# A language adapter with residual layer norm: b2 shared out anew between VectorE and TensorE, and the negative means of two batches in one operation

## The chip, the cores and the metric

The kernel runs on one core of a Trainium2 chip. Its engines work side by side, each through its own instruction queue: TensorE (PE) multiplies matrices, VectorE (DVE) and ScalarE (ACT) work on vectors, GpSimd (POOL) does elementwise work, SyncE (SP) issues the DMAs. The metric is the device time of one execution in microseconds, the median of several runs.

## What is computed

There are 128 sequences ("batches" b) of 128 rows of 512 float32 values. Each has a language id that picks one of ten sets of weights.

```python
h = relu(x @ W1[id] + b1[id])              # 512 -> 128
adapted = h @ W2[id] + b2[id]              # 128 -> 512
y = x + adapted
normed = (y - mean(y)) * rsqrt(var(y) + 1e-05)
out = x + normed * gamma[id] + beta[id]
```

## The kernel before

All weights lie in SBUF from the start; the rows of b2, gamma and beta are spread over 128 partitions (`spread`, line 159). Then one Python loop (line 476), fully unrolled, runs over the steps i. Every engine has its own order of instructions, which is the order of the program: `keep` (line 43) ties each instruction to the one before it on its engine.

In step i, with b = i - 3, the engines work on different batches, as a pipeline:

- TensorE: `transpose_x(i)` (line 202, four transposes), `down(i-1)` (line 225, the first product, eight instructions), `up(i-2)` (lines 236 to 242, the second product, two instructions over 512 columns, into a PSUM tile of the pool `p_y`). `p_y` has five buffers (line 61), so the product of batch b takes the buffer that batch b-5 gave back with its `finish`.
- ScalarE: `copy_xT(i)` (L206), `stage_w1(i+1)` (L197), `relu(i-1)` (L233), `square(b)` (L272, the sum of squares about the mean, which needs the sum of the row), and after every odd b `deviation` (L283, the root of the variance for a pair of batches).
- GpSimd: `add_b2(b+2)` (L212, r = x + b2) and `add_beta(b)` (L219, o = x + beta), 1.28 us each.
- VectorE, in an even step b with g = b / 2 and p = g - 1: `residual(b)` (L257, y = y + r, with the sum of each row as a second result), `rstd_1(p)` (L289), `scale(2p)` (L306, (y - mean) * gamma), `negative_mean(b)` (L263), `rstd_2(p)` (L293), `finish(2p-1)` (L315, o = y * rstd + o), `rstd_3(p)` (L297). In an odd step: `residual(b)`, `rstd_4(p)` (L301), `scale(2p+1)`, `negative_mean(b)`, `finish(2p)`. So batch b-3 is finished in step b. The four `rstd` operations work on two columns, one for each batch of a pair; their results in between lie in a tile `stat` in PSUM (pool `p_s`).

b2 is added in one of three ways. In most batches GpSimd adds it to x (`add_b2`). Where `b2_by_matmul(b)` holds (line 188), TensorE puts it into the PSUM tile with one more matmul ahead of the second product (L241, from bfloat16 parts of the row). Where `b2_by_vector(b)` holds (line 191), VectorE adds it to the product in PSUM (L255) ahead of the residual. In the last two ways the residual takes x itself. Before, 22 batches go to TensorE (0 to 3, and every b with b % 8 == 1, and 5, 117 and 125), 13 to VectorE (b % 8 == 5 from 13 to 109), 93 to GpSimd.

Stores go out by pair of batches (`store`, L319), from SP's queue, which also issues the loads of x, four batches each (L67).

The last four batches (E = 123, so 124 to 127) have an order of their own, written out by hand in `tail` (line 380). There each batch has its own root and reciprocals (`deviation_of` L350 and L352, `rstd_of` with n = 1 to 4, L336, L339, L342, L345, one column each, all in one PSUM tile `stat_ends`). `by_pool` (L366 on ScalarE, L368 and L370 on GpSimd) ends batches 123, 124 and 125, for the first two with `shift` (L360) from the negative mean; `finish_last` (L377) ends 122, 126 and 127 on VectorE. Each is stored by itself (L373).

Of the kernel before, what the change touches and what calls it, by code (L numbers as in the profile page):

```python
# [8 lines left out]
FP = mybir.dt.float32  # L9
# [3 lines left out]
ALU = mybir.AluOpType  # L13
# [3 lines left out]
P = 128  # L17
# [6 lines left out]
def cond_resid_kernel(ctx: ExitStack, tc: tile.TileContext, x, itok, W1, b1, W2, b2, gamma, beta, out):  # L24
# [8 lines left out]
    nc = tc.nc  # L33
    B, S, H = x.shape
# [8 lines left out]
    def keep(ins):  # L43

        engine = ins.ins.engine
        if engine in last:
            tc.add_manual_dep(ins.ins, last[engine], behind, reason="kept order")
        last[engine] = ins.ins.name
        return ins
# [7 lines left out]
    st = ctx.enter_context(tc.tile_pool(name="st", bufs=6))  # L57
    p_x = ctx.enter_context(tc.tile_pool(name="p_x", bufs=1, space=PSUM))
    p_h = ctx.enter_context(tc.tile_pool(name="p_h", bufs=1, space=PSUM))
    p_s = ctx.enter_context(tc.tile_pool(name="p_s", bufs=1, space=PSUM))  # L60
# [109 lines left out]
    lids, xT, w1s, hT, rs, os, ys, ssqs, nmeans, rstds = {}, {}, {}, {}, {}, {}, {}, {}, {}, {}  # L170
    phs, pxs, sums = {}, {}, {}

    def lid(b, engine):
        g = b // G
        if (g, engine) not in lids:
            loads, vals = nc.values_load_multi_w_load_instructions(
                lang[0:1, g * G : (g + 1) * G],
                engines=[engine],
                min_val=0,
                max_val=L - 1,  # L180
                skip_runtime_bounds_check_because="clamped on the chip to 0..L-1 above",
            )
            for ins in loads:
                keep(ins)
            lids[g, engine] = vals
        return lids[g, engine][b % G]
# [2 lines left out]
        return b < 4 or (b % 4 == 1 and not b2_by_vector(b))  # L189

    def b2_by_vector(b):
        return b % 8 == 5 and 8 <= b < B - 16

    def stage_w1(b):
        w1s[b] = wp.tile([P, KC, A], FP, tag="w1s", name=f"w1s_{b}")
# [49 lines left out]
    def col(tiles, b):  # L245

        return tiles[b // 2][:, b % 2 : b % 2 + 1]

    def residual(b):
        r = rs.pop(b) if b in rs else xb(b)  # L250
        if b % 2 == 0:
            sums[b // 2] = st.tile([P, 2], FP, tag="sum", name=f"sum_{b // 2}")
        if b2_by_vector(b):
            v = lid(b, ET.DVE)
            keep(nc.vector.tensor_tensor(ys[b], ys[b], b2_b[:, bass.ds(v * H, H)], ALU.add))  # L255
        keep(
            nc.vector.scalar_tensor_tensor(ys[b], ys[b], 1.0, r, ALU.mult, ALU.add, accum_out=col(sums, b))  # L257
        )

    def negative_mean(b):  # L260
        if b % 2 == 0:
            nmeans[b // 2] = st.tile([P, 2], FP, tag="nmean", name=f"nmean_{b // 2}")
        keep(nc.vector.tensor_scalar(col(nmeans, b), col(sums, b), -1.0 / H, None, ALU.mult))  # L263

    def square(b):

# [10 lines left out]
    sds, y0s, stats = {}, {}, {}  # L277
# [7 lines left out]


    def rstd_1(g):
        y0s[g] = p_s.tile([P, 6], FP, tag="s", name=f"stat_{g}")
        keep(nc.vector.reciprocal(y0s[g][:, 0:2], sds[g]))  # L289

    def rstd_2(g):
        t = y0s[g]
        keep(nc.vector.scalar_tensor_tensor(t[:, 2:4], ssqs.pop(g), EPS * H3, t[:, 0:2], ALU.add, ALU.mult))  # L293
# [9 lines left out]
    def scale(b):  # L303
        v = lid(b, ET.DVE)
        keep(
            nc.vector.scalar_tensor_tensor(  # L306
                ys[b], ys[b], col(nmeans, b), gamma_b[:, bass.ds(v * H, H)], ALU.add, ALU.mult
            )
        )
# [8 lines left out]
    def store(g):  # L318
        nc.sync.dma_start(out=out[2 * g : 2 * g + 2].rearrange("b s h -> s b h"), in_=os.pop(g))  # L319
        del rstds[g]  # L320

    def on(b):
        return 0 <= b < B
# [4 lines left out]
    ends = {}  # L328

    def rstd_of(b, n):  # L330

        if not ends:
            ends["t"] = p_s.tile([P, 32], FP, tag="s", name="stat_ends")
        t = ends["t"][:, 8 * (b % 4) : 8 * (b % 4) + 3]
        if n == 1:
            keep(nc.vector.reciprocal(t[:, 0:1], sds[b]))  # L336
        elif n == 2:
            keep(
                nc.vector.scalar_tensor_tensor(t[:, 1:2], ssqs.pop(b), EPS * H3, t[:, 0:1], ALU.add, ALU.mult)  # L339
            )  # L340
        elif n == 3:
            keep(nc.vector.scalar_tensor_tensor(t[:, 2:3], t[:, 1:2], 1.0 / H3, sds.pop(b), ALU.mult, ALU.add))  # L342
        else:
            rstds[b] = st.tile([P, 1], FP, tag="rstd", name=f"rstd_{b}")
            keep(nc.vector.reciprocal(rstds[b], t[:, 2:3]))  # L345
# [9 lines left out]
    def rstd_col(b):  # L355
        return rstds[b] if b > E else rstds[b // 2][:, b % 2 : b % 2 + 1]
# [15 lines left out]
    def store_last(b):  # L372
        nc.sync.dma_start(out=out[b], in_=os[b // 2][:, b % 2, :])  # L373

    def finish_last(b):
        o = os[b // 2][:, b % 2, :]
        keep(nc.vector.scalar_tensor_tensor(o, ys.pop(b), rstd_col(b), o, ALU.mult, ALU.add))  # L377
        store_last(b)

    def tail(b):  # L380
        p = E // 2
        if b == E + 3:
            rstd_of(b - 2, 3)
        residual(b)
        if b == E + 1:
            rstd_1(p)
            scale(E - 1)
            rstd_2(p)
            negative_mean(b)
            finish(E - 2)  # L390
            store(p - 1)
            rstd_3(p)
            deviation_of(b)
            rstd_4(p)
            shift(E)
            by_pool(E, False)
        elif b == E + 2:
            rstd_of(b - 1, 1)
            negative_mean(b)
            rstd_of(b - 1, 2)  # L400
            finish_last(E - 1)
            store_last(E)
            deviation_of(b)
        elif b == E + 3:
            rstd_of(b - 2, 4)
            shift(b - 2)
            residual(b + 1)
            by_pool(b - 2, False)
            store_last(b - 2)
            rstd_of(b - 1, 1)  # L410
            negative_mean(b)
            rstd_of(b - 1, 2)
            negative_mean(b + 1)
            scale(b - 1)
            deviation_of(b)
            rstd_of(b - 1, 3)
            rstd_of(b - 1, 4)
            scale(b)
            deviation_of(b + 1)
            by_pool(b - 1, True)  # L420
            store_last(b - 1)
            rstd_of(b, 1)
            rstd_of(b, 2)
            rstd_of(b + 1, 1)
            rstd_of(b, 3)
            rstd_of(b + 1, 2)
            scale(b + 1)
            rstd_of(b, 4)
            rstd_of(b + 1, 3)
            rstd_of(b + 1, 4)  # L430
            finish_last(b)
            finish_last(b + 1)


# [41 lines left out]
    for i in range(3, B + U):  # L476
        b = i - U - 1
        if b > 0 and b % G == 0 and b // G + 3 < NG:
            load_x(b // G + 3)
        if i == 4:  # L480
            up(2)
        if i == 5:
            up(3)
        if i > 3 and on(i):
            transpose_x(i)
        if b <= E:
            add_b2(b + 2)
            add_beta(b)
        if i > 4 and on(i - 1):
            down(i - 1)  # L490
        if i > 3 and on(i):
            copy_xT(i)
        if i > 4 and on(i + 1):
            stage_w1(i + 1)
        if i > 4 and on(i - 1):
            relu(i - 1)
        if i > 5 and on(i - U):
            up(i - U)


        g, half = divmod(b, 2)
        p = g - 1
        mine, old = 0 <= p < B // 2, 0 <= p - 1 < B // 2
        if b == E:
            add_b2(b + 3)
            add_beta(b + 1)
            add_b2(b + 4)
            for n in range(b + 2, B):
                add_beta(n)
        if b > E:  # L510
            tail(b)
        elif half == 0:
            if on(b):
                residual(b)
            if mine:
                rstd_1(p)
                scale(2 * p)
            if on(b):
                negative_mean(b)
            if mine:  # L520
                rstd_2(p)
            if old:
                finish(2 * p - 1)
                store(p - 1)
            if mine:
                rstd_3(p)
        else:
            if on(b):
                residual(b)
            if mine:  # L530
                rstd_4(p)
                scale(2 * p + 1)
            if on(b):
                negative_mean(b)
            if mine:
                finish(2 * p)
        if 0 <= b <= E:
            square(b)
            if half == 1:
                deviation(g)  # L540

        for n, engine in ((i + 3, ET.Activation), (i - U + 3, ET.PE), (b + 1, ET.DVE), (b + 5, ET.Pool)):
            if on(n):
                lid(n, engine)
# [37 lines left out]
```

## Time and profile before

| | |
|---|---|
| median of 3 runs | 314.34 us (314.3 to 314.67) |
| the profiled execution | 314.2 us, its span 312.4 us |
| granted TensorE clock, mean | 0.989 |
| L241, b2 by matmul | 22 times |
| L255, b2 on VectorE | 13 times, 690 ns each |
| L263, negative mean | 128 times, 151 ns each |
| L257, residual | 128 times, 693 to 695 ns each |
| L306, scale | 126 times, 743 ns each |
| L315, finish | 122 times, 745 ns each |

The profile is one execution. Its page gives for each engine the busy time, the busy share in 40 equal slices of the span (a digit is tenths), and groups of instructions by line. The timeline gives the start of each instruction, its duration, engine, line and operation; instructions of one engine may overlap in it[...]. "PEld" is TensorE's loading of weights.

### The profile page before, as it was taken

To read this page: it belongs to the slowest core of one execution; us is meant where nothing else is said; L and a number is where in the kernel's file an instruction comes from. 1 tells how busy PE (TensorE), PEld (TensorE's weight loads), DVE (VectorE), ACT (ScalarE), POOL (GpSimd) and SP (SyncE) were. 2 spreads that over 40 slices of the span, in tenths; PEclk is the share of its full clock that TensorE was granted. 3 is DMA by queue.
4 is the path that set the end of the run, shared out by engine and by line. 5 is a ranking of instruction groups with operands and counts; after the bars stand their busy time and mean duration, and the time that the engine had idled before them with its cause. 6 is when DMAs were issued, how large, how long until landed. Compare 5 with 4: busy or idle time off the path is not lost.

```text
span 312.4 us, 7096 instructions
## 1 busy us (share of the span) xinstructions
PE 300.3 (96%) x1870; PEld 222.8 (71%) x1871; DVE 295.6 (95%) x943; ACT 285.8 (91%) x726; POOL 280.1 (90%) x234
## 2 busy tenths in 40 slices
PE   8999999999999999999999999999999999999980
PEld 3566777777777777777777777777777777777740
DVE  6827999999999999999999999999999999999995
ACT  3977999999999999999999999999999999999982
POOL 1307999999999999999999999999999999999964
PEclk9999999999999999999999999999999999999995
DMA  7998678677766667677666667787666667733244
GB/s 208 315 387 317 202 263 271 227 247 269 245 228 234 219 229 266 203 270 270 229 218 213 232 250 244 234 273 268 212 214 213 245 235 236 265 134 129 78 167 168
DMA packets 41001, 72.87 MB, mean 233 GB/s; under 512 B 1753, under 2 KB 6884, under 8 KB 40962
## 3 DMA queue, kind: packets, MB, share of 16 engines
q1 hardware_dynamic: 40902, 72.38, 67.2%
q8 instruction: 15, 0.25, 0.3%
q14 instruction: 24, 0.20, 0.2%
q10 hardware_dynamic: 60, 0.05, 0.1%
HBM read 38.86 MB, written 33.55 MB: 232 GB/s over the span
## 4 chain that ended last, share of the span: by engine, by line
PE 84%; DVE 4%; DMA 4%; SPq 3%; ACT 2%; issue 1%; DVEq 1%; ACTq 0%
PE ph L225 34%; PE py L242 33%; PE pxT L202 17%; DMA w<-in_L_cond_W_dram 4%; SPq L98 2%; PE py L241 1%; DVE py L257 1%; DVE py L306 1%; SPq L84 1%; DVE o L315 1%; ACT sq L350 0%; DVEq L577 0%; ACT xT L206 0%; ACT n L366 0%; ACT sq L272 0%
## 5 line engine op out<-in xcount | busy, mean ns | idle before, releaser
L219 POOL TENSOR_TENSOR o<-x,beta_b 128x512 f32<-128x512 f32 x128 | 162.2, 1280 | 9.1 <-ACT beta_b L166 9.1
L225 PE MATMUL ph<-xT,w1s 128*128 128x128 f32 x1024 | 135.6, 275 | 0.8 <-ACT w1s L197 0.5
L212 POOL TENSOR_TENSOR r<-x,b_b 128x512 f32<-128x512 f32 x93 | 118.9, 1279 | 15.9 <-DMA x<-in_x_dram 11.9
L242 PE MATMUL py<-w,hT 128*128 x256 | 131.2, 594 | 0.5 <-DMA w<-in_L_cond_W_dram 0.5
L225 PEld LDWEIGHTS ph<-xT,w1s 128*128 128x128 f32 x1024 | 124.6, 192 | 3.0 <-ACT hT L233 1.6
L202 PEld LDWEIGHTS pxT<-ident,x 128*128 128x128 f32 x512 | 63.7, 141 | 65.1 <-issue 45.9
L306 DVE SCALAR_TENSOR_TENSOR py<-py,nmean,gamma_b 128x512 f32<-128x512 f32 x126 | 93.6, 743 | 0.0
L315 DVE SCALAR_TENSOR_TENSOR o<-py,rstd,o 128x512 f32<-128x512 f32 x122 | 90.8, 745 | 0.0
L272 ACT ACTIVATE sq<-py,sum 128x512 f32<-128x512 f32 x124 | 85.2, 687 | 2.0 <-DVE py L257 1.8
L206 ACT COPY xT<-pxT 128x512 f32<-128x512 f32 x128 | 73.7, 576 | 9.4 <-PE pxT L202 5.8
L197 ACT COPY w1s<-w 128x512 f32 x128 | 79.3, 620 | 0.2 <-issue 0.2
L202 PE MATMUL pxT<-ident,x 128*128 128x128 f32 x512 | 76.8, 273 | 0.0
L257 DVE SCALAR_TENSOR_TENSOR py<-py,r 128x512 f32<-128x512 f32 x93 | 64.4, 693 | 1.4 <-issue 0.5
L233 ACT ACTIVATE hT<-ph,b1T 128x128 f32<-128x128 f32 x128 | 47.3, 370 | 1.2 <-PE ph L225 1.2
L242 PEld LDWEIGHTS py<-w,hT 128*128 128x128 f32 x256 | 40.5, 192 | 3.2 <-issue 1.6
L257 DVE SCALAR_TENSOR_TENSOR py<-py,x 128x512 f32<-128x512 f32 x35 | 24.3, 695 | 3.8 <-PE py L242 3.3
L272 ACT ACTIVATION_READ_ACCUMULATOR sq<-py,sum 128x1 f32 x124 | 25.6, 207 | 0.0
L283 ACT ACTIVATE sd<-ssq,eps 128x2 f32<-128x2 f32 x62 | 18.3, 296 | 2.1
L263 DVE TENSOR_SCALAR nmean<-sum 128x1 f32<-128x1 f32 x128 | 19.4, 151 | 0.1
L289 DVE RECIPROCAL stat<-sd 128x2 f32<-128x2 f32 x62 | 12.9, 208 | 1.1 <-ACT sd L283 1.1
L257 DVE DVE_READ_ACCUMULATOR py<-py,r 128x1 f32 x93 | 13.3, 143 | 0.0
L301 DVE RECIPROCAL rstd<-stat 128x2 f32<-128x2 f32 x62 | 10.3, 167 | 0.0
(55 smaller groups left out, 111.2 us busy)
## 6 DMA issues: line engine op xcount, KB each, us to landing
out_dram<-o SPq DMA_DIRECT2D x61, 512.0 KB, 3.2
x<-in_x_dram SPq DMA_DIRECT2D x30, 1024.0 KB, 6.0
w<-in_L_cond_W_dram SPq DMA_DIRECT2D x4, 640.0 KB, 6.3
w<-in_L_cond_W_dram SPq DMA_DIRECT2D x2, 1280.0 KB, 11.3
x<-in_x_dram SPq DMA_DIRECT2D x4, 512.0 KB, 8.2
out_dram<-o SPq DMA_DIRECT2D x6, 256.0 KB, 2.0
rows<-in_L_cond_beta_dram ACTq DMA_DIRECT2D x1, 20.0 KB
rows<-in_L_cond_gamma_dram SPq DMA_DIRECT2D x1, 20.0 KB
```

The lines of the kernel that those rows point to most:

```text
L197: keep(nc.scalar.copy(w1s[b].rearrange("p k a -> p (k a)"), src))
L202: keep(nc.tensor.transpose(pxs[b][:, k, :], xb(b)[:, k * P : (k + 1) * P], ident))
L206: keep(nc.scalar.copy(xT[b], pxs.pop(b)))
L212: keep(nc.gpsimd.tensor_tensor(rs[b], xb(b), b2_b[:, bass.ds(v * H, H)], ALU.add))
L219: keep(nc.gpsimd.tensor_tensor(os[g][:, j, :], xb(b), beta_b[:, bass.ds(v * H, H)], ALU.add))
L225: nc.tensor.matmul(phs[b], lhsT=w1s[b][:, k, :], rhs=xT[b][:, k, :], start=(k == 0), stop=(k == KC - 1))
L233: keep(nc.scalar.activation(hT[b], phs.pop(b), AF.Relu, bias=b1T[:, bass.ds(lid(b, ET.Activation), 1)]))
L242: keep(nc.tensor.matmul(ys[b], lhsT=hT[b], rhs=w2[:, bass.ds(v * H, H)], start=not m, stop=True))
L257: nc.vector.scalar_tensor_tensor(ys[b], ys[b], 1.0, r, ALU.mult, ALU.add, accum_out=col(sums, b))
L272: nc.scalar.activation(sq, ys[b], AF.Square, bias=col(sums, b), scale=-float(H), accum_out=col(ssqs, b))
L306: nc.vector.scalar_tensor_tensor(ys[b], ys[b], col(nmeans, b), gamma_b[:, bass.ds(v * H, H)], ALU.add, ALU.mult)
L315: nc.vector.scalar_tensor_tensor(o, ys.pop(b), rstds[g][:, j : j + 1], o, ALU.mult, ALU.add)
```

## The change

`b2_by_vector` holds now for b % 16 in 5, 9 and 13, from 9 to 109: 20 batches; `b2_by_matmul`, which takes what is left of b % 4 == 1, holds for 15. The 93 batches of GpSimd are the same ones.

`negative_mean(b)`, one operation on one column, becomes `negative_means(g)`, one on two columns, after the odd batch of a pair: sums * (-1/512) + 0. Its zeros are two columns of a new PSUM tile `small`, cleared once, in which all small results lie now: those of the pairs (`rstd_1`) in two places in turn, those of the last four batches in four others. `stat` and `stat_ends` are gone.

In `tail` the negative means of 124 and 125 are taken together in the turn of 125, and those of 126 and 127 between `rstd_of(125, 3)` and `rstd_of(125, 4)`. `scale(127)` goes ahead of `rstd_of(126, 2)`, and `finish_last(126)` ahead of `rstd_of(127, 4)`.

```diff
     def b2_by_vector(b):
-        return b % 8 == 5 and 8 <= b < B - 16
+        return b % 16 in (5, 9, 13) and 8 <= b < B - 16
...
-    def negative_mean(b):
-        if b % 2 == 0:
-            nmeans[b // 2] = st.tile([P, 2], FP, tag="nmean", name=f"nmean_{b // 2}")
-        keep(nc.vector.tensor_scalar(col(nmeans, b), col(sums, b), -1.0 / H, None, ALU.mult))
+    small = {}
+
+    def smalls(lo, n):
+        if not small:
+            small["t"] = p_s.tile([P, 64], FP, tag="s", name="small")
+            keep(nc.vector.memset(small["t"][:, 0:2], 0.0))
+        return small["t"][:, lo : lo + n]
+
+    def negative_means(g):
+        nmeans[g] = st.tile([P, 2], FP, tag="nmean", name=f"nmean_{g}")
+        keep(nc.vector.scalar_tensor_tensor(nmeans[g], sums[g], -1.0 / H, smalls(0, 2), ALU.mult, ALU.add))
...
     def rstd_1(g):
-        y0s[g] = p_s.tile([P, 6], FP, tag="s", name=f"stat_{g}")
+        y0s[g] = smalls(8 + 8 * (g % 2), 6)
...
     def rstd_of(b, n):
-        if not ends:
-            ends["t"] = p_s.tile([P, 32], FP, tag="s", name="stat_ends")
-        t = ends["t"][:, 8 * (b % 4) : 8 * (b % 4) + 3]
+        t = smalls(32 + 8 * (b % 4), 3)
...
         if b == E + 1:
             rstd_1(p)
             scale(E - 1)
             rstd_2(p)
-            negative_mean(b)
             finish(E - 2)
...
         elif b == E + 2:
             rstd_of(b - 1, 1)
-            negative_mean(b)
+            negative_means(b // 2)
             rstd_of(b - 1, 2)
...
             rstd_of(b - 1, 1)
-            negative_mean(b)
             rstd_of(b - 1, 2)
-            negative_mean(b + 1)
             scale(b - 1)
             deviation_of(b)
             rstd_of(b - 1, 3)
+            negative_means(b // 2)
             rstd_of(b - 1, 4)
             scale(b)
             deviation_of(b + 1)
             by_pool(b - 1, True)
             store_last(b - 1)
             rstd_of(b, 1)
+            scale(b + 1)
             rstd_of(b, 2)
             rstd_of(b + 1, 1)
             rstd_of(b, 3)
             rstd_of(b + 1, 2)
-            scale(b + 1)
             rstd_of(b, 4)
             rstd_of(b + 1, 3)
+            finish_last(b)
             rstd_of(b + 1, 4)
-            finish_last(b)
             finish_last(b + 1)
...
             if mine:
                 rstd_1(p)
                 scale(2 * p)
-            if on(b):
-                negative_mean(b)
-            if mine:
                 rstd_2(p)
...
             if on(b):
-                negative_mean(b)
+                negative_means(g)
             if mine:
                 finish(2 * p)
```

## The prediction

> **What bounds the kernel now.** I read the busy shares first, then the 40 slices.
>
> ```profile
> PE 300.3 (96%) x1870; PEld 222.8 (71%) x1871; DVE 295.6 (95%) x943; ACT 285.8 (91%) x726; POOL 280.1 (90%) x234
> ...
> PE   8999999999999999999999999999999999999980
> ...
> DVE  6827999999999999999999999999999999999995
> ```
>
> Four engines are over 90% busy and TensorE and VectorE are full in every middle slice, so shares can't tell which of them sets the pace. Starts of the same operation in successive batches can. In the timeline I took TensorE first: the second product (L242) of a batch starts 2.19 us after that of the batch before, and 2.41 us where the batch has a b2 matmul (L241); from batch 5 to 125 only two of 121 distances differ (23 and 24, by 0.08 and 0.10). TensorE sets the pace, evenly. Then VectorE over one even and one odd batch (36 and 37; 37 has its b2 on VectorE):
>
> ```profile
> 101.48 1.02 PE L242 MATMUL py<-w,hT 128*128 x2
> ...
> 102.72 0.69 DVE L257 SCALAR_TENSOR_TENSOR py<-py,r 128x512 f32<-128x512 f32 x1
> ...
> 103.33 0.21 DVE L289 RECIPROCAL stat<-sd 128x2 f32<-128x2 f32 x1
> 103.41 0.74 DVE L306 SCALAR_TENSOR_TENSOR py<-py,nmean,gamma_b 128x512 f32<-128x512 f32 x1
> ...
> 103.67 1.02 PE L242 MATMUL py<-w,hT 128*128 x2
> ...
> 104.06 0.15 DVE L263 TENSOR_SCALAR nmean<-sum 128x1 f32<-128x1 f32 x1
> ...
> 104.12 0.16 DVE L293 SCALAR_TENSOR_TENSOR stat<-ssq,stat 128x2 f32<-128x2 f32 x1
> 104.18 0.74 DVE L315 SCALAR_TENSOR_TENSOR o<-py,rstd,o 128x512 f32<-128x512 f32 x1
> ...
> 104.84 0.16 DVE L297 SCALAR_TENSOR_TENSOR stat<-stat,sd 128x2 f32<-128x2 f32 x1
> ...
> 104.91 0.69 DVE L255 TENSOR_TENSOR py<-py,b_b 128x512 f32<-128x512 f32 x1
> ...
> 105.63 0.70 DVE L257 SCALAR_TENSOR_TENSOR py<-py,x 128x512 f32<-128x512 f32 x1
> ```
>
> The reader is to see two things. First, starts lie closer than durations: L306 lasts 0.74 but the next operation starts 0.65 later, and L263 lasts 0.15 but the next starts 0.06 later. The price of an operation is its **step**, start to next start. Second, the **lag**: residual (L257) of batch 36 starts 0.22 after the end of its product (101.48 + 1.02). I formed this lag for all batches. Its floor is about 0.115 (0.04 in two batches with a b2 matmul), where VectorE waits for TensorE, and it rises by some 0.72 at each batch with b2 on VectorE. At its highest, 1.23 at batch 21, the product of batch 23 was held up, starting 0.054 after finish (L315) of batch 18 had ended: the five buffers of p_y are the other end of the spring. The lag may move between 0.12 and about 1.15; beyond that VectorE stops TensorE.
>
> Mean steps between 40 and 290 us, in ns. Even batch: L257 606, L289 77, L306 649, L263 61, L293 63, L315 661, L297 67: 2.184 us. Odd: 606, L301 82, 649, 61, L315 658: 2.056. Pair 4.240; residual to residual it reads 4.238. A b2 on VectorE adds 0.733 (L255 0.724, and 0.009 behind L257). Eight batches: VectorE 4 x 4.238 + 0.733 = 17.685; TensorE 8 x 2.191 + 0.22 = 17.75. VectorE has 0.06 us in 17.75 to spare.
>
> **What the Trainium skill says.** "Perfetto Trace Analysis", section on the per-instruction lifecycle: the profiled time of a VectorE instruction runs to the write's acknowledgement, while the next may begin its prefetch earlier. The trace agrees: 742 ns against a step of 649. "VectorE: DVE Perf Modes", "The DRAIN you can't avoid": a semaphore after each operation cost nothing extra in its test, so operations are to be saved, not waits. The trace agrees where the awaited result is old (L263 waits and steps in 61 ns), and not where it is fresh: in the last microseconds dependent small operations stand about 200 ns apart. "TensorE: Matmul & The Clock Gate", "Back-to-back issue gap": an isolated 512-column matmul costs about 216 ns; here the b2 matmul lengthens a batch by 220.
>
> **The change, part by part.**
>
> *b2 on VectorE in 20 batches instead of 13, on TensorE in 15 instead of 22.* GpSimd keeps its 93, at the same places (batches 1 in 4 skip it). TensorE loses 7 x 0.22 = 1.5 us. VectorE gains 7 x 0.733 = 5.1 us.
>
> *The paired negative mean.* Per pair two L263 (61 each) go and one SCALAR_TENSOR_TENSOR of 128x2 comes. It is no saving of 302 - 157 as the durations suggest, and not quite one of 61 either: what follows L306 also sets L306's step. Followed by L263 the step is 649; followed by a small SCALAR_TENSOR_TENSOR it is longer, which the end of the trace shows:
>
> ```profile
> 298.72 0.76 DVE L306 SCALAR_TENSOR_TENSOR py<-py,nmean,gamma_b 128x512 f32<-128x512 f32 x1
> ...
> 299.38 0.15 DVE L293 SCALAR_TENSOR_TENSOR stat<-ssq,stat 128x2 f32<-128x2 f32 x1
> ...
> 306.13 0.16 DVE L339 SCALAR_TENSOR_TENSOR stat_ends<-ssq,stat_ends 128x1 f32<-128x1 f32 x1
> ...
> 306.40 0.17 DVE L336 RECIPROCAL stat_ends<-sd 128x1 f32<-128x1 f32 x1
> 306.60 0.17 DVE L342 SCALAR_TENSOR_TENSOR stat_ends<-stat_ends,sd 128x1 f32<-128x1 f32 x1
> 306.81 0.16 DVE L339 SCALAR_TENSOR_TENSOR stat_ends<-ssq,stat_ends 128x1 f32<-128x1 f32 x1
> 306.93 0.76 DVE L306 SCALAR_TENSOR_TENSOR py<-py,nmean,gamma_b 128x512 f32<-128x512 f32 x1
> ```
>
> There L306 to L293 is 662 (the trace's starts to the ns), and L306 to L342 661. L293 has the operands of the new operation: SBUF first, PSUM second, two columns. So the even batch saves 61 and loses 13; the odd one exchanges 649 + 61 for 662 + 63, a loss of 15. Saving: 61 - 13 - 15 = **31 ns a pair**. Bounds: 0 (the new operation costs a further 31) and 61 (neighbours unaffected). Its wait is for the residual's accumulator, over 0.7 old: nothing. Queued behind it are finish and then TensorE's next buffer, which is why its step counts. The wait added at L289 is for results over 1 us old: nothing, hidden under L257's 606.
>
> *Sum, residual of batch 8 to that of 112.* VectorE's work after: 52 pairs x 4.207 = 218.8, 20 x 0.733 = 14.7, together 233.4. Before it was 52 x 4.238 + 13 x 0.733 = 229.9, and the trace has 231.3 (40.22 to 271.55): 1.0 us of waiting for TensorE and 0.4 of two hitches at batches 16 and 56, put down to issue, which I keep. After: 233.8, +2.5. TensorE's own need there is 104 x 2.191 + 6 x 0.22 = 229.2, so from batch 9 VectorE is the bound: per 16 batches 8 x 4.207 + 3 x 0.733 = 35.85 against TensorE's 35.28. The lag rises to the buffers' end and products wait: each block of 16 begins with the lag at about 0.2, adds 0.73 three times and loses 0.35 per four batches, so TensorE is stopped near the second and the third, some 0.2 and 0.38. At 112 the lag stands about 0.2 higher than before (0.59), so TensorE is 2.5 - 0.2 = **2.3 us late**. From 112 on no batch has b2 on VectorE in either kernel; TensorE leads again and the 2.3 stay.
>
> ScalarE's square waits for the residual's sum and moves with it; its relu ends half a us before TensorE wants the buffer, so a lag of 1.5 passes it. GpSimd's sums lie 5 to 9 us ahead. Both cost nothing; if ScalarE's cover were short it would stop TensorE instead of the buffers, for no longer.
>
> *The end.* Taking the negative mean out of batch 124's turn brings all after it forward 0.06: residuals 125 to 127 lag 0.38, 0.30, 0.22, more than 0.115. Two L263 less before scale(125) give 0.01 at most: L339 stands there 0.035 after the reciprocal it needs. The paired operation now sits between L342 and L345 of batch 125. As built it waits for L342 (same PSUM tile), about 0.195, L345 follows, and scale(126) waits for its result: 0.13 lost. scale(127) goes ahead of four small operations, saving nothing in sum, for these stand 200 ns apart wherever they are, each waiting for the one before. From scale(127) at 306.08: 306.74, 307.00, 307.21, 307.41, 307.61, 307.80, finish(126) 307.89 (before 308.08); rstd_of(127,4) 308.56, and finish(127) must wait 0.27 for it: 308.83 against 308.75. Its store is the last on SP's queue, and batch 125's before it still waits for GpSimd. End: **+0.1**, bounds -0.3 and +0.3.
>
> Total 2.3 + 0.1 = +2.4. The profiled execution took 314.2 (span 312.4 and 1.8 around it), so 316.6; on the median of 314.34, 316.7.
>
> **The rivals.** *A, forecast*, 0.74: 315.4 to 317.8. *B, faster*: the paired operation frees VectorE by more than its neighbours show. If it saves 103 ns a pair (36.10 - 35.28 over 8), VectorE fits under TensorE; then 7 x 0.22 comes off and the time is 312.9. At 77 ns it breaks even. For it speak the listed durations (302 against about 157); against it the steps. 0.07. *C, nothing saved*: the new operation waits or steps longer; 52 x 0.031 = 1.6 more, 318.3. 0.11. *D, no change*: saving 61, no hitches and 0.3 won at the end: +2.4 - 1.6 - 0.4 - 0.3 = +0.1, 314.4. 0.08.
>
> **How the numbers follow.** 0.2% (0.63 us) is about what a measurement of this kernel can tell from no change. B is faster, D the same, A and C slower: 0.07, 0.08, 0.85. The range leaves out B and D (0.15): from 315.0, where the saving is 61 with the hitches kept, to 318.4, where it is 0.
>
> **What would show it.** Right: TensorE's products held up by finish near batches 27, 31, 43, 47 and so on, VectorE without idle time from 9 to 112, pair steps of 4.207, residual 112 some 2.5 later. Wrong: an even 2.19 on TensorE throughout (B), pair steps at 4.24 (C) or under 4.18 (D), or an end that moves by over 0.3 from residual 127 to the last store.

## The result, and the profile after

The changed kernel takes 315.88 us (median of 6 runs, 315.77 to 316.3) against 314.40 (6 runs) for the kernel before, run beside it: ratio 1.0045, 95% interval 1.0034 to 1.0057. It is slower. The profiled execution took 315.87 us with a span of 314.1 (before 314.2 and 312.4). First the page of the changed kernel, the lines that were read of before: busy time by engine, then the slices of TensorE and VectorE.

```profile
PE 301.5 (96%) x1864; PEld 222.6 (71%) x1864; DVE 297.1 (95%) x887; ACT 287.1 (91%) x726; POOL 280.3 (89%) x234
...
PE   8999999999999999999999999999999999999970
...
DVE  6827999999999999999999999999999999999995
```

The page shows next to nothing of the difference. VectorE has 56 instructions fewer and is busy 1.5 us longer; these slices differ in one digit. Differences of starts tell it, as they did before. I cut the span at the ends of the second products (L242) of batches 8, 112 and 125, and at the start of the last finish:

| us | before | after | difference |
|---|---|---|---|
| start to product 8 | 40.11 | 40.30 | +0.19 |
| product 8 to product 112 ("the stretch") | 230.86 | 232.08 | +1.22 |
| product 112 to product 125 | 29.35 | 29.36 | +0.01 |
| product 125 to the last finish ("the end") | 8.43 | 8.71 | +0.28 |
| last finish to the end of the span | 3.68 | 3.66 | -0.02 |

The first row is not the change's: in the runs below it lies anywhere between 39.88 and 40.58, without order. The second is the forecast mechanism, in the timeline of the changed kernel around the product of batch 31 (L314 is scale, L323 finish, L271 the paired mean, L297, L301, L305 and L309 the four rstd operations; before they were L306, L315, L263, L289, L293, L297 and L301):

```profile
88.80 0.74 DVE L314 SCALAR_TENSOR_TENSOR py<-py,nmean,gamma_b 128x512 f32<-128x512 f32 x1
...
89.45 0.15 DVE L271 SCALAR_TENSOR_TENSOR nmean<-sum,small 128x2 f32<-128x2 f32 x1
...
89.51 0.74 DVE L323 SCALAR_TENSOR_TENSOR o<-py,rstd,o 128x512 f32<-128x512 f32 x1
...
90.17 0.69 DVE L257 SCALAR_TENSOR_TENSOR py<-py,r 128x512 f32<-128x512 f32 x1
90.31 0.30 PEld L242 LDWEIGHTS py<-w,hT 128*128 128x128 f32 x2 [0.26 <-DVE o L323]
90.31 1.12 PE L242 MATMUL py<-w,hT 128*128 x2
...
92.61 1.02 PE L242 MATMUL py<-w,hT 128*128 x2
```

Finish of batch 26 ends at 89.51 + 0.74 = 90.25, and 0.06 later the product of batch 31 starts, which takes its buffer. It starts 2.43 us after product 30 instead of 2.19, itself takes 1.12 instead of 1.02, and the next one follows 2.29 behind: 0.34 lost at one place. TensorE is stopped so around products 15, 27, 31, 43, 47, 59, 63, 75, 79, 91, 95, 107 and 111, 2.93 us in sum (before: 0.18). The 2.75 more, less the 1.54 that TensorE is spared by seven b2 matmuls, are the 1.2 us by which the stretch is longer. The lag of the residual behind its product climbs to 1.39 at batches 29, 45 and so on, and is back at its floor of 0.108 at 20, 36, 52, 84 and 100.

VectorE's steps in the loop of the changed kernel: scale to L271 647.5 ns on average (52 times), scale to L301 650 (52 times), L271 to finish 62.7; a pair takes 4.180 us without waiting, 58 ns less than before.

### The profile page after: what moved, and what is told of

Read it like the earlier page. It is cut to its first block, busy times and chain, and to the rows that moved or that the text cites. A ratio compares the mean times of both kernels' runs of the same rounds, so it can differ in the third digit from the quotient of the medians.

```text
span 314.1 us, 7091 instructions
## 1 busy us (share of the span) xinstructions
PE 301.5 (96%) x1864; PEld 222.6 (71%) x1864; DVE 297.1 (95%) x887; ACT 287.1 (91%) x726; POOL 280.3 (89%) x234
## 4 chain that ended last, share of the span: by engine, by line
PE 63%; DVE 17%; issue 9%; DMA 4%; SPq 3%; DVEq 2%; ACT 1%; ACTq 0%
PE py L242 26%; PE ph L225 24%; PE pxT L202 12%; DVE py L257 5%; DVE py L314 4%; DMA w<-in_L_cond_W_dram 4%; DVE o L323 3%; SPq L98 2%; DVEq L176 2%; DVE py L255 1%; SPq L84 1%; PE py L241 1%; DVE small L305 1%; DVE nmean L271 1%; DVE o L383 1%
## 5 line engine op out<-in xcount | busy, mean ns | idle before, releaser
L242 PE MATMUL py<-w,hT 128*128 x256 | 132.3, 599 | 0.9 <-DMA w<-in_L_cond_W_dram 0.4
L314 DVE SCALAR_TENSOR_TENSOR py<-py,nmean,gamma_b 128x512 f32<-128x512 f32 x126 | 93.9, 745 | 0.3 <-issue 0.2
L323 DVE SCALAR_TENSOR_TENSOR o<-py,rstd,o 128x512 f32<-128x512 f32 x122 | 91.4, 749 | 0.0
L257 DVE SCALAR_TENSOR_TENSOR py<-py,r 128x512 f32<-128x512 f32 x93 | 64.6, 695 | 0.7 <-POOL r L212 0.2
L242 PEld LDWEIGHTS py<-w,hT 128*128 128x128 f32 x256 | 39.9, 191 | 4.6 <-DVE o L323 1.8
L257 DVE SCALAR_TENSOR_TENSOR py<-py,x 128x512 f32<-128x512 f32 x35 | 24.4, 698 | 3.8 <-PE py L242 2.9
L297 DVE RECIPROCAL small<-sd 128x2 f32<-128x2 f32 x62 | 13.0, 210 | 1.3 <-ACT sd L291 1.3
L255 DVE TENSOR_TENSOR py<-py,b_b 128x512 f32<-128x512 f32 x20 | 13.9, 695 | 0.0
L257 DVE DVE_READ_ACCUMULATOR py<-py,r 128x1 f32 x93 | 13.5, 145 | 0.0
L309 DVE RECIPROCAL rstd<-small 128x2 f32<-128x2 f32 x62 | 10.5, 169 | 0.0
```

Source lines behind the costliest of these rows:

```text
L242: keep(nc.tensor.matmul(ys[b], lhsT=hT[b], rhs=w2[:, bass.ds(v * H, H)], start=not m, stop=True))
L314: nc.vector.scalar_tensor_tensor(ys[b], ys[b], col(nmeans, b), gamma_b[:, bass.ds(v * H, H)], ALU.add, ALU.mult)
L323: nc.vector.scalar_tensor_tensor(o, ys.pop(b), rstds[g][:, j : j + 1], o, ALU.mult, ALU.add)
```

## The experiments

Every ratio is to the kernel before on the same chip, from five rounds, with its 95% interval. "Stretch" and "end" are the rows of the table.

**The paired mean and the new end, with the old share of b2.**

```diff
-        return b % 16 in (5, 9, 13) and 8 <= b < B - 16
+        return b % 8 == 5 and 8 <= b < B - 16
```

> The changed kernel with the old rule for b2 (13 batches on VectorE, 22 on TensorE), so the paired negative mean and the new end alone. Theory (VectorE's rate over batches 9 to 112 is what the change made longer): with 2 batches of b2 per 16 VectorE needs 8 x 4.18 + 2 x 0.74 = 34.9 us per 16 batches and TensorE 35.5, so TensorE leads everywhere, no product waits for finish, and batches 8 to 112 take 230.7 us as before (less its one stop of 0.18). The end keeps the 0.28 us that it lost. Time 314.4 to 314.7. Rival (the paired operation over zeros in PSUM is what costs, by its step or its waits): 315.9 as in the changed kernel, with VectorE's pair step over 4.24.

Measured: 314.40 us, ratio 1.0011 (1.0002 to 1.0019); stretch 230.68, no stop at all, end 8.70. The 58 ns a pair (3.0 us in 52 pairs) that VectorE is spared shorten the stretch by 0.18, the two hold-ups of before. TensorE sets it. The end is as long as in the changed kernel, though no product was held up here.

**The new share of b2 alone**, everything else as before:

```diff
-        return b % 8 == 5 and 8 <= b < B - 16
+        return b % 16 in (5, 9, 13) and 8 <= b < B - 16
```

> The kernel before with the new rule for b2 alone (20 batches on VectorE, 15 on TensorE); negative means one by one and the old end. Theory with the saving that the changed kernel shows, 58 ns a pair: VectorE needs 2 x 17.685 + 0.733 = 36.1 us per 16 batches where the changed kernel took 35.7, so 6 x 0.4 and 0.2 in the first batches come on top and the 0.28 of the end goes: 318.2. With the forecast's saving of 31 ns a pair: 317.2. Rival (the paired operation is what costs): faster than the changed kernel, 314.4 or below.

Measured: 318.07 us, ratio 1.0125 (1.0110 to 1.0139); stretch 234.54, 14 products held, 5.4 us in sum (13 and 2.9 in the changed kernel), end 8.44. VectorE's need from residual 8 to 112 is 52 x 4.238 + 20 x 0.733 = 235.0; the trace has 235.2. The stretch is 2.46 longer than in the changed kernel, which has the same share: that is what the paired mean is worth where VectorE is the bound, 47 ns a pair; the rest of the 58 went in the changed kernel into slightly dearer additions of b2, a longer hitch and longer steps where VectorE has caught up with TensorE, all reckoned below. 31 ns is too little.

**The end alone undone**: the changed loop, with the negative means of batches 124 to 127 one by one, in the old order, and the small results of these four batches in a PSUM tile of their own (four, as before, not two as the expectation has it).

```diff
-        t = smalls(32 + 8 * (b % 4), 3)
+        if not ends:
+            ends["t"] = p_s.tile([P, 32], FP, tag="s", name="stat_ends")
+        t = ends["t"][:, 8 * (b % 4) : 8 * (b % 4) + 3]
...
-            negative_means(b // 2)
+            negative_mean(b)
```

> The changed kernel with the last batches' small operations as before (one negative mean per batch, the last two batches' small results in a tile of their own); the loop keeps the paired mean and the new share of VectorE. The theory (the end alone costs 0.28 us, because the paired operation, the reciprocal and the step after it share one PSUM tile): from the product of batch 125 to the last finish 8.44 us instead of 8.71, the stretch from batch 8 to 112 unchanged at 232.1 with the same stops, the whole 1.0036 times the kernel before, 0.28 us under the changed one. Rival (the 8.71 is left over from the lateness of VectorE at batch 112): the end stays at 8.7 and the time at 1.0045.

Measured: 315.49 us, ratio 1.0044 (1.0030 to 1.0057); stretch 232.09, end 8.44. In the trace the end is 0.27 shorter than in the changed kernel with the same stretch, as the theory had it. The ratio doesn't show it: 1.0044 is the rival's figure, and its interval, 0.8 us wide, covers both. The next run has a narrower one.

**The paired mean alone**: old share, old end.

> The old share of VectorE (2 in 16) and the old end; only the paired mean in the loop is left of the change. The theory (TensorE sets the stretch when VectorE has 2 in 16, so that 58 ns per pair saved on VectorE buy nothing): stretch 230.7, end 8.44, ratio 1.000 (within 0.001). Rival (the saving shortens the way to the end too): ratio 0.999 or less, 0.3 us or more under the kernel before.

Measured: 314.07 us, ratio 0.9995 (0.9987 to 1.0004); stretch 230.68, end 8.45. Against the first experiment, which differs in the end only, the ratio is lower by 0.0016 (0.5 us; the intervals just overlap) and the end in the trace shorter by 0.25, at the same stretch. So the end's 0.28 comes from the new end, not from lateness before it. The paired mean alone buys nothing in the trace: the stretch is that of the first experiment, and the end that of before. The times by themselves don't exclude the rival, whose 0.999 lies inside the interval.

**Where the end loses it.** The timeline of the changed kernel, VectorE in the turn of batch 125 and at the very end (L342, L345, L348 and L351 are the four `rstd_of`, L383 the last finishes):

```profile
302.67 0.21 DVE L342 RECIPROCAL small<-sd 128x1 f32<-128x1 f32 x1
302.91 0.16 DVE L271 SCALAR_TENSOR_TENSOR nmean<-sum,small 128x2 f32<-128x2 f32 x1
303.10 0.17 DVE L345 SCALAR_TENSOR_TENSOR small<-ssq,small 128x1 f32<-128x1 f32 x1
303.19 0.75 DVE L383 SCALAR_TENSOR_TENSOR o<-py,rstd,o 128x512 f32<-128x512 f32 x1
...
309.51 0.75 DVE L383 SCALAR_TENSOR_TENSOR o<-py,rstd,o 128x512 f32<-128x512 f32 x1
310.17 0.16 DVE L351 RECIPROCAL rstd<-small 128x1 f32<-128x1 f32 x1
310.45 0.75 DVE L383 SCALAR_TENSOR_TENSOR o<-py,rstd,o 128x512 f32<-128x512 f32 x1
```

The same turn in the timeline of before (L336 and L339 are the first two `rstd_of`, L263 the negative mean):

```profile
301.30 0.21 DVE L336 RECIPROCAL stat_ends<-sd 128x1 f32<-128x1 f32 x1
301.48 0.15 DVE L263 TENSOR_SCALAR nmean<-sum 128x1 f32<-128x1 f32 x1
301.55 0.16 DVE L339 SCALAR_TENSOR_TENSOR stat_ends<-ssq,stat_ends 128x1 f32<-128x1 f32 x1
```

After, L271 starts 0.24 behind L342 and L345 0.19 behind L271, where before the negative mean stood 0.18 behind the reciprocal and the next operation only 0.07 behind that. L342 is `rstd_of(124, 1)`. L271, the means of 124 and 125, takes nothing from it; what the two share is the PSUM tile `small`, which holds the zeros that L271 reads and the result that L342 writes. L345 takes a result from L342 alone, which is 0.43 old when it starts.

If the shared tile is what makes the last operations wait, tiles of their own should free them. Tiles in SBUF, one for each of the last four batches:

```diff
...
-        t = smalls(32 + 8 * (b % 4), 3)
+        if n == 1:
+            own[b] = st.tile([P, 3], FP, tag="own", name=f"own_{b}")
+        t = own[b]
```

> The changed kernel with the small results of each of batches 124 to 127 in an SBUF tile of its own, so that no operation of one batch waits for one of another; order of instructions as in the changed kernel. Theory (the end is slow because every small operation waits for the last user of one shared tile): 0.19 comes back in the turn of 125, 0.13 ahead of scale(126), and the chain from scale(127) to finish of 126, six operations 0.2 apart, halves: another 0.5. Time 315.1. Rival (the 0.2 are the time for a result to be seen by the next operation of the same batch, whatever the tile): 0.2 at most, 315.7.

Measured: 316.70 us, ratio 1.0080 (1.0067 to 1.0093); the end is 9.79, 1.08 longer instead of shorter; both expectations missed. Its timeline, VectorE (L347 is the second `rstd_of` there) and GpSimd:

```profile
307.68 2.48 POOL L378 TENSOR_TENSOR o<-n,o 128x512 f32<-128x512 f32 x2
...
309.24 0.94 DVE L347 SCALAR_TENSOR_TENSOR own<-ssq,own 128x1 f32<-128x1 f32 x1
310.11 0.15 DVE L344 RECIPROCAL own<-sd 128x1 f32<-128x1 f32 x1
```

A one-column operation that lasts 0.15 elsewhere in this run lasts 0.94 and ends at 310.18, 0.02 after GpSimd's two sums (307.68 + 2.48 = 310.16). It has two tensors in SBUF now; with one of them in PSUM it didn't wait. The third `rstd_of` of batches 124 and 125 does the same, with 0.73 and 0.70 (from 303.73 and 306.92). But the steps behind the long operation are about 0.1 apart (310.11, 310.22, 310.29, 310.41, 310.49), not 0.2, and in the turn of 125 L271 starts 0.17 behind the reciprocal and the next operation 0.08 behind L271, nearly as before the change. So the shared tile's waits are real, and this cure brought longer ones. The same results in the same tiles, with the second operand given as a pointer to a scalar per partition instead of a tensor:

```diff
...
-                nc.vector.scalar_tensor_tensor(t[:, 1:2], ssqs.pop(b), EPS * H3, t[:, 0:1], ALU.add, ALU.mult)
+                nc.vector.tensor_scalar(t[:, 1:2], ssqs.pop(b), EPS * H3, t[:, 0:1], ALU.add, ALU.mult)
...
-            keep(nc.vector.scalar_tensor_tensor(t[:, 2:3], t[:, 1:2], 1.0 / H3, sds.pop(b), ALU.mult, ALU.add))
+            keep(nc.vector.tensor_scalar(t[:, 2:3], t[:, 1:2], 1.0 / H3, sds.pop(b), ALU.mult, ALU.add))
```

> The changed kernel with the small results of batches 124 to 127 in SBUF tiles of their own and the two operations on them as TENSOR_SCALAR with the second operand as a pointer to one value per row, so that none has two tensors in SBUF. Theory (in the run with own tiles two effects were mixed: the shared tile's waits went, and an operation with two SBUF tensors waits for GpSimd's running one): no wait for GpSimd, the chain from scale(127) to finish of 126 in steps near 0.1: last finish 7.9 us after the product of 125 where the changed kernel has 8.71, so 0.8 below the changed kernel. Rival (results in SBUF are slow for these operations however they are written): 9.8 us as with own tiles, 1 us above the changed kernel.

Measured: 315.55 us, ratio 1.0041 (1.0028 to 1.0054). The end is 8.11, shorter by 0.60; nothing waits for GpSimd. But from the last finish to the end of the span it is 4.04 instead of 3.66: the stores of batches 125, 126 and 127 now start within 1.0 us instead of 1.5, and 0.38 of the 0.60 is given back there. The 0.2 that is left is too little for the ratio to show.

**The same price in the loop.** The zeros in SBUF instead of PSUM:

```diff
+    zeros = const.tile([P, 2], FP, name="zeros")
+    nc.gpsimd.memset(zeros, 0.0)
...
-        keep(nc.vector.scalar_tensor_tensor(nmeans[g], sums[g], -1.0 / H, smalls(0, 2), ALU.mult, ALU.add))
+        keep(nc.vector.scalar_tensor_tensor(nmeans[g], sums[g], -1.0 / H, zeros, ALU.mult, ALU.add))
```

> The changed kernel with the two columns of zeros in SBUF, not in the PSUM tile of the other small results. Theory: the place of the zeros means nothing for the step (pair 4.18 as with PSUM), so batches 8 to 112 keep their 232.1 us; but in the turn of batch 125 the paired operation and the one behind it no longer wait for the last user of that tile, which gives back 0.19: 315.7. Rival (two operands in SBUF make the step longer, which is why the zeros were put into PSUM): 13 ns a pair is 0.7 more, 316.4; 30 ns is 317.2.

Measured: 355.89 us, ratio 1.1308 (1.1282 to 1.1335), out of the reach of both expectations. The timeline of that kernel, GpSimd's sum and the paired mean (L272 there), twice:

```profile
150.74 1.28 POOL L221 TENSOR_TENSOR o<-x,beta_b 128x512 f32<-128x512 f32 x1
151.16 0.88 DVE L272 SCALAR_TENSOR_TENSOR nmean<-sum,zeros 128x2 f32<-128x2 f32 x1
...
155.92 1.27 POOL L214 TENSOR_TENSOR r<-x,b_b 128x512 f32<-128x512 f32 x1
156.09 1.12 DVE L272 SCALAR_TENSOR_TENSOR nmean<-sum,zeros 128x2 f32<-128x2 f32 x1
```

Both times the small operation ends 0.02 after GpSimd's (152.04 and 152.02, 157.21 and 157.19). It lasts 802 ns on average instead of 153, though only 43 of the 64 wait at all; 52 times 0.65 makes 33.7 of the 35.2 us by which the stretch is longer. The Trainium skill states the rule, in "SBUF — State Buffer", section "Who interferes with whom": a VectorE instruction with two SBUF inputs contends with a GpSimd instruction that reads SBUF; the lock is exclusive, and the order of issue decides which of the two waits. The two waits shown agree. One other goes beyond it: the operation at 40.14 lasts 4.55 us and ends 0.02 after the fourth GpSimd operation in a row, of which three had started after it. Why these went ahead is not known; the wait held finish, and behind it TensorE's next product, which waited 3.95 us. The section names `tensor_scalar` as another that may do so, in its modes with two ports. So the paired mean in that form, without zeros at all:

```diff
-        keep(nc.vector.scalar_tensor_tensor(nmeans[g], sums[g], -1.0 / H, smalls(0, 2), ALU.mult, ALU.add))
+        keep(nc.vector.tensor_scalar(nmeans[g], sums[g], -1.0 / H, None, ALU.mult))
```

> The changed kernel with the paired negative mean as one TENSOR_SCALAR of 128x2, SBUF to SBUF, without zeros. Theory (only two tensors in SBUF make VectorE wait for GpSimd): as the changed kernel, 0.2 better at the end, where it no longer waits for the shared tile. Rival (a TENSOR_SCALAR on an even number of float32 values in SBUF reads over both ports, and waits for GpSimd too, as the Trainium skill has it for such modes): 62 waits of 0.6 us, as with zeros in SBUF, some 40 us slower.

Measured: 355.75 us, ratio 1.1287 (1.1255 to 1.1319), L271 813 ns on average (64 times, of which 43 wait, one of them 4.55 us): the rival came true, with fewer waits than it reckoned. The one-column form of before is the same operation on the same tiles and lasts 151. So the zeros in PSUM are no detour: of the three forms of the two-column mean they are the only one that doesn't wait for GpSimd.

**Other shares.** If VectorE is short by 3 in 16 and has room at 2 in 16, 2.5 in 16 could fit (old end, paired mean in the loop):

```diff
-        return b < 4 or (b % 4 == 1 and not b2_by_vector(b))
+        return b < 4 or (b % 32 in (1, 14, 21) if 8 <= b < B - 16 else b % 4 == 1)
...
-        return b % 16 in (5, 9, 13) and 8 <= b < B - 16
+        return b % 32 in (4, 10, 17, 23, 30) and 8 <= b < B - 16
```

> The paired negative mean in the loop, the end of the kernel before, and b2 on VectorE in 5 of 32 batches, 6 or 7 apart (16 between 8 and 112), by TensorE in 3 of 32. Theory: VectorE needs 16 x 4.18 + 5 x 0.74 = 70.6 us per 32 batches and TensorE 32 x 2.191 + 3 x 0.22 = 70.8, and as VectorE's batches with b2 stand apart the lag is back at its floor before each: no product waits, batches 8 to 112 take 230.9 - 0.18 - 3 x 0.22 = 230.0 us, 0.8 less than in the kernel before, and the end is as before: 0.8 below it. Rival (VectorE is the bound as soon as more b2 goes to it): no gain, at or above the kernel before.

Measured: 314.30 us, ratio 1.000 (0.9992 to 1.0008); stretch 230.95. No product waits for a buffer. But the transposes of batches 36, 68, 80, 100 and 112 come late, and the second products behind them start 0.92 us late in sum (without the b2 matmuls of batches 78 and 110, which fall there). That is all by which the stretch misses the 230.0 of the theory. In each of the five, TensorE's queue holds a load of the language ids of 1.16 to 1.23 us (the one for batch 80 runs from 191.64 to 192.87, and the transposes start at 193.05, 0.27 later than 2.19 behind those before). Three more loads as long (for 44, 52 and 76) stopped nothing. The id loads on TensorE's queue in that kernel (shortest, median and longest in ns):

```profile
L176 PEldq TENSOR_LOAD <-lang x32: 328/604/1225, 20.6 to 289.3; - x32
```

The same share at other places, so that GpSimd skips the same batches as before:

```diff
-        return b % 16 in (5, 9, 13) and 8 <= b < B - 16
+        return b % 32 in (5, 9, 17, 21, 29) and 8 <= b < B - 16
```

> Five of 32 batches to VectorE (5, 9, 17, 21, 29) and three to TensorE (1, 13, 25), so that GpSimd skips the same batches as before; paired mean in the loop, old end. VectorE needs 8 x 4.18 + 2.5 x 0.74 = 35.29 us per 16 batches, TensorE 35.50 - 0.11 = 35.39. If only the number per 16 counts: 0.71 us less than before in the stretch (230.0), ratio 0.998. If two at a distance of four batches already fill the five buffers, as batches 21 and 25 did in the changed kernel (a stop of 0.10 us each pair): six or seven stops of 0.1 us give it back, stretch 230.6, ratio 0.9995 to 1.000. If what failed at other places (late transposes behind slow loads of the language ids) comes here too: stretch 231 or more, ratio above 1.001.

Measured: 314.18 us, ratio 0.9998 (0.9990 to 1.0007); stretch 230.60, end 8.46. The id loads are short again:

```profile
L176 PEldq TENSOR_LOAD <-lang x32: 328/332/777, 20.5 to 289.2; - x32
```

And six products are held, 0.10 each, at 24, 44, 56, 76, 88 and 108, always behind the second of two batches on VectorE that stand four apart. The timeline of that kernel (L328 is finish):

```profile
71.62 0.74 DVE L328 SCALAR_TENSOR_TENSOR o<-py,rstd,o 128x512 f32<-128x512 f32 x1
...
72.43 1.12 PE L242 MATMUL py<-w,hT 128*128 x2
...
74.72 1.02 PE L242 MATMUL py<-w,hT 128*128 x2
```

Finish of batch 18 ends at 72.36; product 23 starts 0.06 later, takes 1.12 and puts off the next by 0.10. That is the second of the three cases written down, to the tenth: 0.7 us spared on TensorE, 0.6 given back to the buffers. In the trace the stretch is 0.26 shorter than before, which the ratio can't tell from nothing.

**Twenty, spread evenly.** To part the number of batches from their crowding, 20 on VectorE every five or so:

```diff
-        return b < 4 or (b % 4 == 1 and not b2_by_vector(b))
+        return b < 4 or (b in (17, 33, 49, 64, 80, 98) if 8 <= b < B - 16 else b % 4 == 1)
...
-        return b % 16 in (5, 9, 13) and 8 <= b < B - 16
+        return b in (9, 14, 19, 25, 30, 35, 40, 45, 51, 56, 61, 66, 71, 77, 82, 87, 92, 97, 103, 108)
```

> The changed kernel with its 20 batches of b2 on VectorE spread evenly, 5 or 6 apart, and TensorE's 6 between them; nothing else. Theory (VectorE's rate over the stretch is the bound, not the crowding of three such batches in nine): 52 x 4.18 + 20 x 0.74 = 232.2 us of VectorE's work remain, so TensorE is still stopped, and only what VectorE idles at the floor before each crowd goes: batches 8 to 112 take 231.5 to 231.9 instead of 232.1. Rival (the crowding is what stops TensorE, the spring of five buffers being too short for it): the stops go and the stretch falls to TensorE's own 229.2, 2.5 us below the changed kernel.

Measured: 328.15 us, ratio 1.0433 (1.0408 to 1.0458), stretch 237.87; both expectations missed. Two waits of that kernel that the changed one doesn't have (us in sum, times, longest):

```profile
POOL o L219 <- DMA out_dram<-o: 20.7, 11, 3.5
...
DVE py L257 <- POOL r L212: 8.0, 13, 2.9
```

GpSimd waits for stores to give back its o tiles, and VectorE for GpSimd's r. The batches that GpSimd skips no longer fall one in each group of four. That its sums so come later against the loads of x, which on SP's queue stand ahead of the stores, is likely but not tested. The test is not clean: it moved a third engine, and says nothing on crowding.

## Why the prediction was right, and where its sum was off

The forecast was slower, 316.7 with a range of 315.0 to 318.4; it is 315.88.

- *VectorE becomes the bound from batch 9*: shown. Products stop at finish, near 27, 31, 43, 47 as written and also at 15. The stops are 0.10 and 0.34 each, forecast 0.2 and 0.38. With the old share they are gone (first experiment); with the new share alone nearly the same products stop for almost twice as long (second).
- *b2 on VectorE costs 0.733*: 0.740 in the changed kernel (L255 to L257 729 ns instead of 724).
- *The paired operation saves 31 ns a pair*: this is the step that failed, and most of the error. The prediction took it that the follower sets the step of scale (L306), 649 ahead of L263 and 662 ahead of a small SCALAR_TENSOR_TENSOR, and read that off two instances in the last microseconds, those at 298.72 and at 304.29. In the loop of the changed kernel scale steps 647.5 ahead of exactly such an operation. The 662 belongs to scale itself, which lasts 752 ns or more in some places: in the trace of before, 13 scales followed by L263 do so too, and step 661 to 667. In 12 of the 13, and at 298.72 as well, the residual ahead stands at the floor of the lag (0.115 to 0.119): VectorE had caught up with TensorE. One of them, in the timeline of before:

```profile
227.52 0.75 DVE L306 SCALAR_TENSOR_TENSOR py<-py,nmean,gamma_b 128x512 f32<-128x512 f32 x1
228.19 0.15 DVE L263 TENSOR_SCALAR nmean<-sum 128x1 f32<-128x1 f32 x1
```

  So the loss of 13 and 15 ns isn't there, and the saving is 58 (4.238 - 4.180). Over 52 pairs the 27 ns more are 1.40 us.
- *Sum, residual 8 to 112*: forecast 233.8, measured 232.70. The 1.40 goes off; 0.14 comes on for the 0.740; one hitch of 0.25 (batch 68) stands for the 0.4 that the forecast kept; and 0.32 is left over, which the forecast didn't have. Some 0.24 of it are longer steps right behind residuals 8, 20, 36, 52, 84 and 100, which stand at the floor of the lag (the steps behind each are about 0.04 longer together). -1.40 + 0.14 - 0.15 + 0.32 = -1.09. The 0.4 itself was read too low: by their steps (1085 and 898 ns from finish to residual, where 658 is usual) the two hitches of before are 0.67, and the waiting for TensorE 0.8 instead of 1.0.
- *Lag at 112 0.2 higher*: 0.726 against 0.585, so 0.14. TensorE was forecast 2.3 late and is 1.22.
- *ScalarE and GpSimd cost nothing*: no product waits for either in the changed kernel.
- *The end, +0.1*: +0.28, near the upper bound. The order of the last operations came as forecast (finish(126), then rstd_of(127, 4) 0.67 later, then 0.27 of waiting). What failed is an omission: the prediction charged the paired operation of batches 126 and 127, which waits behind `rstd_of(125, 3)`, but not that of 124 and 125, which waits in the same way behind `rstd_of(124, 1)` and makes `rstd_of(124, 2)` wait for it (0.19).
- *Rivals*: B needed 103 ns a pair to be faster, and 77 to break even; it has 58. C needed 0. D's saving of 61 was nearly right, but not its other two terms (a hitch stayed, and the end lost 0.28); the time lies between A's middle and D.

Two errors of opposite sign, 1.1 in the stretch and 0.2 in the end, left the forecast 0.8 high.

What the hitches are, the trace does show in part. Every four batches VectorE's queue loads the language ids of the next four (L176, about 0.82 us, mostly hidden behind finish). The load before residual 68 of the changed kernel lasts 0.90, from 173.33 to 174.23, and the residual starts 0.16 behind it; the two hitches of before stand 0.16 behind loads of 1.42 and 0.88 us. Why these loads come late or last longer isn't shown, and a wait of 0.36 ahead of a scale in the turn of batch 118, after the stretch, has no load beside it.

Open: why scale lasts 752 to 760 ns in some batches. In the even turns it does so wherever the residual stands at the floor of the lag, in the changed kernel and in the run with 5, 9, 17, 21 and 29 of 32 without exception (14 of 62 scales ahead of rstd_2 in the one, a single one of them off the floor, and 23 of 62 in the other); nothing here was made to test what the one has to do with the other. That a batch of GpSimd's at another place lengthens TensorE's id loads is seen in one pair of runs, and its mechanism isn't. Whether 20 evenly spread batches would have stopped TensorE less was tried only in the run that disturbed GpSimd.

## What to carry to other kernels

When two engines both fill the span, compare what each needs per period, in steps from start to start, and see how far the spring between them (here five buffers) reaches: work moved from the one to the other costs nothing only while the taker has room, and then its price less that room (5.1 us of b2 moved alone made the stretch 3.7 us longer); and even with room in the sum, work that comes crowded can fill the spring, as two batches four apart did. Read a step from many instances at equal duration of the first instruction; a few at the end of a trace can belong to another state. Small results that are used at the same time belong in different tiles, and a small VectorE operation with two tensors in SBUF, or a two-column TENSOR_SCALAR, doesn't belong beside a busy GpSimd.

## What was unexpected of the hardware

- The small two-column mean lasts 153 ns with its second input in PSUM, 802 with both in SBUF and 813 as a TENSOR_SCALAR, when GpSimd is busy all the time; it ends 0.02 us after GpSimd's running operation. Once it waited through four GpSimd operations, 4.55 us. The one-column TENSOR_SCALAR lasts 151 beside the same GpSimd. Against the changed kernel the waits cost some 40 us.
- A chain of small VectorE operations steps at about 0.2 us in one PSUM tile and at about 0.12 where two such chains alternate in SBUF tiles of their own (308.05, 308.17, 308.29, 308.42, 308.54, 308.66 in the run with pointers).
- A product whose buffer comes back 0.06 before it starts takes 1.12 us instead of 1.02.
- A load of four language ids takes 0.33 us on TensorE's queue in most groups and up to 1.2 in others, and about 0.82 on VectorE's; in the late cases above the engine's next instruction started 0.16 to 0.18 us behind its end.
